# A four-layer graph network on one core: operands filled to 128 rows and columns, readers after all writers of a bank, and a new order

## The chip, the cores and the metric

The kernel runs on one core of a Trainium2 chip. The metric is the device time of one execution in microseconds (us): the median of the runs, 2941.53 us before the change (3 runs, 2940.82 to 2942.3).

A core has five engines with a queue of instructions each: TensorE (PE in the profile; PEld is its loading of weights), VectorE (DVE), ScalarE (ACT), GpSimd (POOL) and SyncE (SP), which only issues DMAs here. TensorE writes to PSUM, eight banks of 128 x 512 fp32; VectorE and ScalarE read them.

## The reference

There are B = 32 graphs with 512 nodes of 128 features and a 512 x 512 adjacency of zeros and ones (3% ones). Four layers follow each other, each on relu(layernorm(x)) = h and each added to x:

```python
# layer 0: p = h @ (W1 - W2), q = h @ W2; maximum over a node's neighbours
x = x + max_j(relu(p[i] + q[j] + b) * adj[i, j])
# layer 1: four inner layers, with earlier inputs concatenated to the third's and fourth's
src = nodes @ ws + bs;  src_agg = l2norm(adj, rows) applied to src
dst = nodes @ wd + bd;  dst_agg = l2norm(adj, columns), transposed, applied to dst
nodes = tanh(concat(src_agg, nodes @ wn + bn, dst_agg) @ wu + bu)
# layer 2: rows of adj divided by their sums
x = x + (adj / rowsum) @ (h @ weight) + bias
# layer 3: four gated recurrent (GRU) steps with m = adj.T @ (h @ weight[l])
r, z = sigmoid(...), sigmoid(...);  n = tanh(xn + r * hn);  h = (1 - z) * n + z * h
```

## The kernel before

**One graph after another, six at a time.** `batch(b)` writes down the work of one graph: `load`, `prepare` (layer 0's projections, the transposed adjacency `at`, the neighbours' ranks `ccd`, row and column sums), `gathers` (layer 0's maximum), `layer1`, `layer23`. Nothing is issued there: `F.vec`, `F.act`, `F.pool`, `F.sync`, `F.mm` and `F.tr` only note operations in a `Flow`. `Flow.run` is a planner that works when the program is built. It keeps up to AHEAD = 6 parts (the weights' three parts, then graphs) open, and picks instruction after instruction: of those whose inputs and buffers are ready first on an engine, the one with the earliest due time. So each engine's queue is a fixed order in which several graphs' work is mixed, and TensorE's products of one graph fill another's waits. The profile gives nearly all work the line of the call in `Flow.step`, L510.

**Due times.** An operation's due time is its graph's place times `PACE`, less the planned length of what follows it in its graph, less its stage's `LEADS`: a higher lead means earlier. `FIRST` and `LAST` shift the places of the first and last graphs, `WEIGHTS` are the places of the weights' parts. The costs in `Flow.cost` are the planner's own estimates. `spaced` keeps the maxima of gathered rows SPACING apart. Where the planner sees a long gap on TensorE it puts in "spin" products, whose result nobody reads.

**Banks.** All products go to eight PSUM banks, which four groups share: group 0 is `prepare`, 1 is `layer1`, 2 is layers 2 and 3, 3 is `gathers`. `BANKS` says how many each group is sure of; the rest are spare, for any group.

**Layer 0.** For rank k = 1 to 4, `oh` marks where a half of the nodes has its k-th neighbour, and `pa = qhl.T @ oh` fetches that neighbour's q by a product; VectorE takes the maximum into `acc`. The neighbours that are left (up to seven a node) are fetched by indirect DMAs, `G<-qtab,idx`, into the maximum `gm`.

**Layer 1.** The features are split into an fp32r high part and a low part, `hi` and `lo`, which are multiplied by the exact 0/1 matrices `at` and `an` into `pg`; `ag` is `pg` times the norms `rbc`. All weights of an inner layer are multiplied together ahead of time, so that `pu` sums fp32 products of features (`f`, `hT`) and aggregates (`ag`). What the biases `bs` and `bd` add depends on the node through its sums of the normalized adjacency: that is one fp32r product of the weights `b8` (8 x 128: high and low parts) and `rows` (8 x 512), the first into each `pu`:

```python
F.mm(flat(pu), W.b8[:, i, :], rows, start=True, stop=False)
```

`rows` comes from `sc`, six columns of scalars for each node (four of them the high and low parts), which GpSimd computes in `prepare`, TensorE transposes (`psc`, a tile of 128 x 24), ScalarE copies to `sct`, and SP writes to DRAM and reads back as rows.

**Layer 2.** `po` is one bank with four fp32 products, one for each 128 nodes; VectorE reads each of its quarters into `x` (x3 in the code). The tile framework keeps a bank's writers and readers apart by waits, in the order in which they were issued; the planner sees only each quarter.

**Layer 3.** In each step l, `pk` are the two gates, `pg` the aggregate that ScalarE copies to `mT`, `phn` and `pxn` the candidate's two products; `ph` is the transposed new state, of which `hi` and `lo` are made for the next step, or `xo` at the end. Only the last graph (`own`) is cut in halves of 256 nodes (`cuts`), takes its banks from group 0 and its buffers from stages that are done, so that it overlaps with the one before it. Its halves share the bank of `phn` (with `pxn` in the same bank) and that of `ph`.

Of the kernel before, what the change touches and what calls it, by code (L numbers as in the profile page):

```python
# [24 lines left out]
P = 128  # L25
# [8 lines left out]
NLEFT = 7  # L34
PACE = 45.35
SPACING = 1.8
AHEAD = 6
BANKS = (2, 1, 2, 1)

LEADS = {  # L40
    "prepare": -33.2, "counts": -28.6, "keys": -38.2, "rows": -9.6,
    "gather0": 12.6, "gather1": -3.5, "gather2": -1.7, "gather3": -10.5,
    "first": 14.4, "layer1": -15.5, "layer10": -39.2, "layer11": -39.2,
    "layer12": -26.1, "layer13": -57.9, "layer2": 50.7, "layer3": 187.5,
    "layer30": 155.2, "layer31": 193.8, "layer32": 81.5, "layer33": 66.2,
    "out": 33.8,
}
FIRST = (-0.01, -0.0, -0.31, 0.0)
LAST = (0.0, -0.23, -0.17, -0.97, -0.05)
WEIGHTS = (-5.87, -1.69, -2.33)  # L50

# [204 lines left out]
class Engine:  # L256
# [5 lines left out]
    def __getattr__(self, op):  # L262
        fn = getattr(self.real, op)

        def note(*args, **kw):
            outs, ins = [], []
            for i, v in enumerate(args):
                (outs if i == 0 else ins).append(v)
            for k, v in kw.items():
                (outs if k in ("out", "accum_out") else ins).append(v)  # L270
            ins = [v.ap if isinstance(v, Rows) else v for v in ins]
            outs, ins = ([v for v in vs if hasattr(v, "free_size")] for vs in (outs, ins))
            cost, after = self.flow.cost(self.name, op, outs, ins)
            self.flow.note(self.name, fn, args, kw, outs, ins, cost, after)


            tensors = [v for v in ins if v.free_size() >= 64 and in_sbuf(v)]
            fast = self.name == "vec" and op == "tensor_scalar" and outs[0].free_size() > 256
            if self.name == "vec" or (self.name == "pool" and op.startswith("tensor")):
                self.flow.part[-1].port = fast or len(tensors) > 1  # L280

        return note


class Flow:
# [50 lines left out]
    def cost(self, engine, op, outs, ins):  # L336

        aps = outs + ins
        n = max(a.free_size() for a in aps)
        o = outs[0].free_size()  # L340
        if "dma" in op:
            if engine != "pool":
                width = 2 if outs[0].dtype == BF16 else 4
                return 0.48 if engine == "sync" else 0.42, 2.0 + outs[0].size() * width / 1.2e5
            return (1.25, 6.0) if "indirect" in op else (0.7, 4.0)
        if engine == "vec":
            if op == "tensor_scalar" and o > 256:
                t = o / 1920.0 + 0.157
            elif op == "bn_stats":
                t = 0.28  # L350
            else:
                t = (o if op != "max" else n) / 960.0 + 0.15
                if op == "scalar_tensor_tensor" and len(ins) == 3:
                    t += 0.06
            return t - 0.082 + (0.08 if len(outs) > 1 else 0.0), 0.082
        if engine == "act":
            t = o / 1200.0 + 0.16 + 0.1 * (len(ins) - 1) + (0.04 if in_sbuf(ins[0]) else 0.0)
            return t - 0.1 + (0.2 if len(outs) > 1 else 0.0), 0.1
        if op == "tensor_tensor" and o < 64:
            return 1.1 if o < 8 else 1.7, 0.0  # L360
        two = op in ("tensor_tensor", "tensor_add", "tensor_sub", "tensor_mul")
        return (o / 408.0 + 0.05 if two and o > 64 else o / 1100.0 + 0.18), 0.0
# [35 lines left out]
    def mm(self, out, lhsT, rhs, start, stop, group=None):  # L398

        n = rhs.free_size()  # L400
        if rhs.dtype == F32:
# [7 lines left out]

    def tr(self, out, in_, ident):  # L410
        self.note(
            "pe", self.nc.tensor.transpose, (out, in_, ident), {}, [out], [in_, ident],
            0.109 if in_.dtype == F32 else 0.056, 0.16,
# [190 lines left out]
class FastWeights:  # L604
# [5 lines left out]
    def __init__(self, nc, F, a, const, mid, ps):  # L610
# [47 lines left out]
        nc.gpsimd.memset(self.sign[0:4, 1:2], 0.0)  # L658
        self.nc, self.a, self.const, self.n = nc, a, const, n

    def own(self, shape, dtype, name):
        return self.F.tile(self.const, shape, dtype, name, name)

    def temp(self, tag, name, wide=False):
# [27 lines left out]
    def rest(self):  # L692
# [30 lines left out]

        self.b8 = self.own([8, NL1, P], F32R, "b8r")
        bm = self.own([P, NL1, 2, 8], F32, "bm")
# [5 lines left out]
        for i in range(NL1):  # L731
# [24 lines left out]
            for k in range(2):  # L756
# [10 lines left out]
            F.vec.scalar_tensor_tensor(  # L767
                self.b8[:, i, :], hi.bitcast(F32), self.sign[0:8, 0:1], full, ALU.mult, ALU.add
            )
# [53 lines left out]
def fast(ctx: ExitStack, tc: tile.TileContext, a: dict, out: bass.AP, bad):  # L823
# [12 lines left out]
    F.share(ps, 8, {f"ps{s}": n for s, n in enumerate(BANKS)} | {"idle": 0})  # L836

    def bank(s, shape, dtype, name):
        return F.tile(ps, shape, dtype, f"ps{s}", name, BANKS[s])

# [54 lines left out]

    def transposed(s, src, name):

        pt = pst(s, name)
        for t in range(NT):
            F.tr(pt[:, t, :], src[:, t, :], W.ident)  # L900
        return pt

# [7 lines left out]

    def parts(s, src, tag, buf=plain, cuts=(slice(None),)):

        hi = buf(F32R, f"hi{s}", f"hi_{tag}")
        lo = buf(F32R, f"lo{s}", f"lo_{tag}")
        for c in cuts:
            v, h, l = ((w if len(cuts) == 1 else w[:, c, :]) for w in (src, hi, lo))
            F.act.copy(h, v)
# [13 lines left out]
    def prepare(b, xt, af):  # L931
# [60 lines left out]
        for t, (first, step) in enumerate(CODES):  # L992
            F.sync.dma_start(
                out=tab[first : first + (P - 1) * step + 1 : step, :], in_=qn[:, t, :]
            )
        F.lead = LEADS["counts"]

# [14 lines left out]

        F.lead = LEADS["keys"]


        dm = F.tile(small, [P, 2, NT], F32, tag="dm", name=f"dm_{b}", bufs=4)
        F.pool.tensor_scalar(dm, deg, 1.0, None, ALU.max)
        sc = F.tile(small, [P, 6, NT], F32, tag="sc", name=f"sc_{b}", bufs=4)
        F.pool.tensor_tensor(
# [34 lines left out]
        pt = pst(0, f"psc_{b}")  # L1054
        F.tr(pt[0 : 6 * NT, 0, :], sc.rearrange("p k t -> p (k t)"), W.ident)
        sct = F.tile(small, [6 * NT, P], F32, tag="sct", name=f"sct_{b}", bufs=1)
# [6 lines left out]
    def gathers(b, at, ccd, qhl, pn, tab, idx, has, dinv):  # L1063
# [15 lines left out]
        for jt in range(NT):  # L1079
            F.lead = LEADS[f"gather{jt}"]  # L1080
            for k in range(1, KSLOT + 1):
                oh = F.tile(big, [P, 2, N], F32R, tag="oh", name=f"oh_{b}_{jt}_{k}", bufs=3)
                F.vec.tensor_scalar(oh, ccd[jt], NBASE + k, None, ALU.is_equal)
                for u in range(2):
# [4 lines left out]
                    else:  # L1089
                        F.vec.tensor_max(acc, acc, flat(pa))  # L1090
        F.lead = LEADS["first"]
        pt = transposed(3, acc.rearrange("p (t q) -> p t q", q=P), f"px_{b}")
# [15 lines left out]
    def layer1(b, x1, an, at, dinv):  # L1108
# [5 lines left out]
        F.sync.dma_start(out=rbc, in_=scal[0:2, :].unsqueeze(0).to_broadcast([P, 2, N]))  # L1114
        rows = F.tile(mid, [8, N], F32R, tag="rows", name=f"rows_{b}")

        xn = norm(1, x1, f"{b}_1")
        two = sbuf_parts(1, xn, f"{b}_1")
        F.act.copy(rows, row8)
        pt = transposed(1, xn, f"pt_{b}_1")  # L1120
# [5 lines left out]
        for i in range(NL1):  # L1126
            F.lead = LEADS[f"layer1{i}"]
            names = INPUTS[i]
# [10 lines left out]
            pu = pst(1, f"pu_{b}_{i}")  # L1139
            F.mm(flat(pu), W.b8[:, i, :], rows, start=True, stop=False)  # L1140
            late = []
# [13 lines left out]
            feat[new] = fi  # L1155
        F.lead = LEADS["layer2"]
        pt = transposed(1, feat[new], f"px_{b}_2")
# [5 lines left out]
    def layer23(b, x2, an, at, dinv):  # L1163
# [16 lines left out]
        for t in range(NT):  # L1180
            F.mm(po[:, t, :], mT[:, t, :], W.w2, start=True, stop=True)
        x3 = x2
        F.lead = LEADS["layer3"]
        for t in range(NT):
# [15 lines left out]
        for l in range(W.NL3):  # L1200
            F.lead = LEADS[f"layer3{l}"]
            gates = []
# [42 lines left out]
            else:  # L1245
                halves = [(v[:, 0:step, :], v[:, step:NT, :]) for v in phn]
            pt = pst(s, f"ph_{b}_{l}")
            for c, (vh, vx) in zip(cuts, halves):
                F.mm(flat(vh), W.gh[l][:, 2, :], flat(cut(h, c)), start=True, stop=True)
                F.vec.scalar_tensor_tensor(  # L1250
                    cut(nn, c), vh, W.bhh[:, n : n + 1], cut(r, c), ALU.add, ALU.mult
                )
                F.mm(flat(vx), W.gm[l][:, 2, :], flat(cut(mT, c)), start=True, stop=True)
                F.vec.tensor_add(cut(nn, c), vx, cut(nn, c))
# [7 lines left out]
                for t in range(c.start, c.stop):  # L1262
                    F.tr(pt[:, t, :], hn[:, t, :], W.ident)
            h = hn
            if l + 1 < W.NL3:
                two = parts(2, pt, f"{b}_3_{l}", buf, cuts)
        F.lead = LEADS["out"]
        xo = buf(F32, "mT", f"xo_{b}")
        for t in range(NT):
            c = b * NT + t  # L1270
            F.vec.scalar_tensor_tensor(
                xo[:, t, :], pt[:, t, :], W.mcol[:, c : c + 1], x3[:, t, :], ALU.mult, ALU.add
            )
# [3 lines left out]
    def batch(b):  # L1277
        F.lead = LEADS["prepare"]
        one = prepare(b, *load(b))
        F.lead = LEADS["rows"]  # L1280
        one = gathers(b, *one)
        F.lead = LEADS["layer1"]
        layer23(b, *layer1(b, *one))
# [486 lines left out]
```

## Time and profile before

| What | Before |
|---|---|
| Median of 3 runs | 2941.53 us |
| Profiled execution | 2943.54 us |
| Its span, first to last instruction | 2941.8 us |
| Instructions | 37748 |
| Granted TensorE clock, mean | 0.993 of full speed |
| PE products, busy | 2843.4 us, 11493 |
| VectorE, busy | 2384.2 us, 5382 |
| ScalarE, busy | 1218.1 us, 2547 |
| GpSimd, busy | 1827.3 us, 2013 |
| The 8-row product `pu<-rows,b8r` | 128, mean 493 ns |
| The transposition `psc<-ident,sc` | 32, mean 273 ns |
| Layer 2's `po<-w,mT` | 256 passes, mean 288 ns in the table by form |

The span is the time between the first and the last instruction of the profiled execution, which lasted 1.7 us longer. A row like `PE pu<-ag,w 128*128 128x512` names the engine, the tile that is written, what it is made from, the weights' shape (rows*columns) and the moving operand's shape. An fp32 product runs as two passes and shows as two instructions. A matmul's record overlaps with the next one's: what it costs is read from start to start.

### The profile page before, as it was taken

To read this page: it belongs to the slowest core of one execution; us is meant where nothing else is said; L and a number is where in the kernel's file an instruction comes from. 1 tells how busy PE (TensorE), PEld (TensorE's weight loads), DVE (VectorE), ACT (ScalarE), POOL (GpSimd) and SP (SyncE) were. 2 spreads that over 40 slices of the span, in tenths; PEclk is the share of its full clock that TensorE was granted. 3 is DMA by queue.
4 is the path that set the end of the run, shared out by engine and by line. 5 is a ranking of instruction groups with operands and counts; after the bars stand their busy time and mean duration, and the time that the engine had idled before them with its cause. 6 is when DMAs were issued, how large, how long until landed. Compare 5 with 4: busy or idle time off the path is not lost.

```text
span 2941.8 us, 37748 instructions
## 1 busy us (share of the span) xinstructions
PE 2843.4 (97%) x11493; PEld 1753.8 (60%) x11513; DVE 2384.2 (81%) x5382; ACT 1218.1 (41%) x2547; POOL 1827.3 (62%) x2013
## 2 busy tenths in 40 slices
PE   7899999999999999999999999999999999999997
PEld 3555556666666566666666566666666666555555
DVE  6988878888888898888888888889888888887533
ACT  2434434434444344344444444444344444333323
POOL 4676667666666666666666666666666666565312
PEclk8999999999999999999999999999999999999999
DMA  7642434334334334333433433343333333342100
GB/s 154 145 91 48 84 69 86 85 72 81 65 66 86 85 74 86 59 72 80 86 85 73 84 61 65 86 87 77 80 68 69 75 86 84 56 77 37 33 4 9
DMA packets 191267, 218.44 MB, mean 74 GB/s; under 512 B 30376, under 2 KB 139600, under 8 KB 191056
## 3 DMA queue, kind: packets, MB, share of 16 engines
q0 software_dynamic: 47104, 92.34, 22.2%
q1 hardware_dynamic: 73768, 63.63, 7.4%
q10 hardware_dynamic: 70184, 59.98, 6.7%
q8 instruction: 93, 1.52, 0.2%
q14 instruction: 118, 0.97, 0.1%
HBM read 164.32 MB, written 17.96 MB: 62 GB/s over the span
## 4 chain that ended last, share of the span: by engine, by line
PE 80%; DVE 10%; issue 4%; DMA 2%; ACT 2%; POOL 1%; ACTq 0%; SPq 0%; DVEq 0%; POOLq 0%
PE pg L510 25%; PE pu L510 19%; PE pk L510 15%; PE pa L510 6%; PE phn L510 4%; PE pxn L510 3%; DVE acc L510 3%; PE pkey L510 2%; PE ph L510 2%; PE pf L510 2%; PE po L510 1%; DMA G<-qtab,idx 1%; DVE nn L510 1%; PE pt L510 1%; DVE x L510 1%
## 5 line engine op out<-in xcount | busy, mean ns | idle before, releaser
L510 POOL DMA_INDIRECT G<-qtab,idx x768 | 848.6, 1105 | 589.6 <-DVE gm L510 453.3
L510 DVE TENSOR_TENSOR acc<-acc,pa 128x512 f32<-128x512 f32 x992 | 673.6, 679 | 146.4 <-PE pa L510 134.5
L510 PE MATMUL pa<-oh,qhl 128*128 128x512 f32 x1024 | 465.7, 510 | 11.2 <-DVE oh L510 5.3
L510 PE MATMUL pg<-an,hi 128*128 128x512 f32 (+1 forms) x1040 | 457.3, 441 | 0.6 <-DVE acc L510 0.4
L510 PE MATMUL pu<-ag,w 128*128 128x512 f32 x896 | 448.0, 592 | 0.5 <-DVE ag L510 0.3
L510 PE MATMUL pg<-an,lo 128*128 128x512 f32 (+1 forms) x1040 | 436.0, 422 | 0.0
L510 DVE TENSOR_SCALAR oh<-ccd 128x1024 fp32r<-128x1024 bf16 x512 | 393.9, 787 | 13.3 <-PE pa L510 13.2
L510 PE MATMUL pg<-at,lo 128*128 128x512 f32 x640 | 295.9, 462 | 0.8 <-DVE lo L510 0.4
L510 PE MATMUL pg<-at,hi 128*128 128x512 f32 x640 | 281.1, 439 | 7.2 <-DVE acc L510 1.8
L510 PEld LDWEIGHTS pa<-oh,qhl 128*128 128x128 f32 x1024 | 193.9, 191 | 152.2 <-issue 40.4
L510 ACT ACTIVATE xn<-x,shift,rstd 128x128 f32<-128x128 f32 x512 | 211.5, 484 | 171.6 <-POOL shift L510 170.1
L510 DVE TENSOR_TENSOR gm<-gm,G 128x128 f32<-128x128 f32 x768 | 253.4, 331 | 8.7 <-DMA G<-qtab,idx 7.7
L510 PE MATMUL pk<-h,g_hh 128*128 128x512 f32 (+1 forms) x528 | 256.3, 590 | 0.6 <-DVE top L510 0.6
L510 PEld LDWEIGHTS pg<-an,hi 128*128 128x128 f32 x1040 | 195.1, 188 | 93.2 <-issue 49.1
L510 PEld LDWEIGHTS pg<-an,lo 128*128 128x128 f32 x1040 | 195.2, 188 | 84.7 <-issue 40.3
L510 PE MATMUL pk<-mT,g_ih 128*128 128x512 f32 (+1 forms) x528 | 242.3, 580 | 1.4 <-ACT mT L510 1.1
L510 ACT ACTIVATE gate<-pk,bsum 128x512 f32<-128x512 f32 (+1 forms) x264 | 176.9, 673 | 140.8 <-PE pk L510 137.3
L510 PEld LDWEIGHTS pu<-ag,w 128*128 128x128 f32 x896 | 168.1, 189 | 110.9 <-issue 80.0
L510 POOL TENSOR_TENSOR rstd<-rstd,mhalf 128x4 f32<-128x4 f32 x128 | 139.8, 1092 | 138.8 <-DVE shift L510 133.6
L510 DVE TENSOR_TENSOR ag<-pg,rbc 128x512 f32<-128x512 f32 x256 | 174.8, 684 | 61.3 <-PE pg L510 58.5
L510 ACT COPY mT<-pg 128x512 f32<-128x512 f32 (+1 forms) x164 | 94.2, 575 | 304.6 <-PE pg L510 300.0
L510 ACT CAST hi<-ph 128x512 fp32r<-128x512 f32 (+1 forms) x99 | 56.8, 574 | 341.2 <-PE ph L510 333.4
(172 smaller groups left out, 5110.4 us busy)
## 6 DMA issues: line engine op xcount, KB each, us to landing
af<-in_adj_dram ACTq DMA_DIRECT2D x32, 1024.0 KB
ccd<-cc SPq DMA_DIRECT2D x512, 64.0 KB
an<-in_adj_dram POOLq DMA_DIRECT2D x128, 256.0 KB, 3.9
x<-in_x_dram ACTq DMA_DIRECT2D x64, 256.0 KB
rbc<-scal SPq DMA_DIRECT2D x32, 512.0 KB
G<-qtab,idx POOLq DMA_INDIRECT x768, 3.8
qtab<-qn SPq DMA_DIRECT2D x128, 64.0 KB
out_dram<-xo ACTq DMA_DIRECT2D x32, 256.0 KB
```

What stands on the lines that cost most here:

```text
L510: op.fn(*(real(v) for v in op.args), **{k: real(v) for k, v in op.kw.items()})
```

## The change

It does four things.

- **Filled operands.** `b8` becomes 128 x 4 x 128 and `rows` 128 x 512, filled with zeros once at the start; only their first 8 partitions are written afterwards. `rows` is one fixed buffer instead of a tile of its own ring, which had one buffer too. `sc` becomes the first 24 columns of one of two fixed 128 x 128 tiles (`vectors`, zero elsewhere), and the whole tile is transposed.
- **Layer 2's projections.** The four products into `po` are noted as writers of the whole bank, so that the planner issues every reader after all of them.
- **Halves.** In the last graph each half's `ph` has its own bank, and both products of a half's candidate are issued before their first reader.
- **The order.** New `PACE`, `SPACING`, `BANKS`, `LEADS`, `FIRST`, `LAST` and `WEIGHTS`; the first and the last graph get leads of their own, which are added to the stage's. [...]

```diff
-PACE = 45.35
-SPACING = 1.8
+PACE = 47.93
+SPACING = 1.5
-BANKS = (2, 1, 2, 1)
+BANKS = (2, 1, 3, 1)
 LEADS = {
...
-    "layer12": -26.1, "layer13": -57.9, "layer2": 50.7, "layer3": 187.5,
-    "layer30": 155.2, "layer31": 193.8, "layer32": 81.5, "layer33": 66.2,
-    "out": 33.8,
+    "layer12": 4.8, "layer13": -92.9, "layer2": -3.0, "layer3": -37.4,
+    "layer30": 11.6, "layer31": 120.9, "layer32": 146.5, "layer33": 18.4,
+    "out": 39.3,
 }
-FIRST = (-0.01, -0.0, -0.31, 0.0)
-LAST = (0.0, -0.23, -0.17, -0.97, -0.05)
-WEIGHTS = (-5.87, -1.69, -2.33)
+LEADS0 = {
...
+LEADSN = {
...
+    "layer12": 77.8, "layer13": 256.2, "layer2": 230.7, "layer3": 341.4,
+    "layer30": 205.3, "layer31": 82.3, "layer32": 56.8, "layer33": 15.6,
...
+FIRST = (9.02, 0.15, 0.05, 0.0)
+LAST = (0.0, -0.06, -0.82, -0.98, -9.3)
+WEIGHTS = (-8.07, -5.76, -16.24)
...
+    def lead(b, stage):
+        own = LEADS0 if b == 0 else LEADSN if b == B - 1 else {}
+        return LEADS[stage] + own[stage] if stage in own else LEADS[stage]
...
-            fast = self.name == "vec" and op == "tensor_scalar" and outs[0].free_size() > 256
+            fast = self.name == "vec" and op == "tensor_scalar"
...
-            return (1.25, 6.0) if "indirect" in op else (0.7, 4.0)
+            return (1.05, 6.0) if "indirect" in op else (0.7, 4.0)
...
+        self.rows = self.zeros([P, n // P, P], "rows")
+        self.vectors = []
+        for i in range(2):
+            t = fixed([P, P], F32, f"vectors{i}")
+            nc.gpsimd.memset(t, 0.0)
+            self.vectors.append(F.fixed(t, [P, P], F32))
...
+    def zeros(self, shape, name):
+        t = self.const.tile(shape, F32R, name=name)
+        for k in range(shape[1]):
+            self.nc.vector.tensor_scalar(t[:, k, :], self.ident, 0.0, None, ALU.mult)
+        return self.F.fixed(t, shape, F32R)
...
-        self.b8 = self.own([8, NL1, P], F32R, "b8r")
+        self.b8 = self.zeros([P, NL1, P], "b8r")
...
-        sc = F.tile(small, [P, 6, NT], F32, tag="sc", name=f"sc_{b}", bufs=4)
+        full = W.vectors[b % 2]
+        sc = full[:, 0 : 6 * NT].rearrange("p (k t) -> p k t", t=NT)
...
-        F.tr(pt[0 : 6 * NT, 0, :], sc.rearrange("p k t -> p (k t)"), W.ident)
+        F.tr(pt[:, 0, :], full, W.ident)
...
-        F.act.copy(rows, row8)
+        F.act.copy(flat(W.rows[0:8]), row8)
...
-            F.mm(flat(pu), W.b8[:, i, :], rows, start=True, stop=False)
+            F.mm(flat(pu), W.b8[:, i, :], flat(W.rows), start=True, stop=False)
...
-            F.mm(po[:, t, :], mT[:, t, :], W.w2, start=True, stop=True)
+            F.mm(po[:, t, :], mT[:, t, :], W.w2, start=True, stop=True, group=po)
...
-            pt = pst(s, f"ph_{b}_{l}")
-            for c, (vh, vx) in zip(cuts, halves):
-                F.mm(flat(vh), W.gh[l][:, 2, :], flat(cut(h, c)), start=True, stop=True)
+            pts = [pst(s, f"ph_{b}_{l}_{c.start}") for c in cuts]
+            for c, (vh, vx), bank_, pt in zip(cuts, halves, phn, pts):
+                bank_ = bank_ if len(cuts) > 1 else None
+                F.mm(
+                    flat(vh), W.gh[l][:, 2, :], flat(cut(h, c)), start=True, stop=True, group=bank_
+                )
+                F.mm(
+                    flat(vx), W.gm[l][:, 2, :], flat(cut(mT, c)), start=True, stop=True, group=bank_
+                )
                 F.vec.scalar_tensor_tensor(
                     cut(nn, c), vh, W.bhh[:, n : n + 1], cut(r, c), ALU.add, ALU.mult
                 )
-                F.mm(flat(vx), W.gm[l][:, 2, :], flat(cut(mT, c)), start=True, stop=True)
```

`LAST` has five entries of which the code uses the first four: those of the last four graphs.

## The prediction

> **What bounds the kernel now.** I read the page first: which engine is full, and where.
>
> ```profile
> PE 2843.4 (97%) x11493; PEld 1753.8 (60%) x11513; DVE 2384.2 (81%) x5382; ACT 1218.1 (41%) x2547; POOL 1827.3 (62%) x2013
> PE   7899999999999999999999999999999999999997
> DVE  6988878888888898888888888889888888887533
> ```
>
> TensorE is full in all but the first and last slice, VectorE never for long. The chain that ended last, in order of time, shows how regular it is:
>
> ```profile
> 1141.88 3.19 PE pu L510 x7
> ...
> 1228.43 3.19 PE pu L510 x7
> ...
> 1314.99 3.19 PE pu L510 x7
> ```
>
> The same piece comes back every 86.55 us, a batch's period. 32 periods are 2770 us; 172 of the span's 2941.8 us lie in the filling and draining ends. The stages by time:
>
> ```profile
> 50.00:100.00 50.00, 42.02 (x205) 22.85 (x206) 46.23 (x112) 15.06 (x41) 34.62 (x42) 0.84 0.84 137
> 1000.00:2000.00 1000.00, 990.80 (x4032) 617.44 (x4031) 849.97 (x1921) 436.53 (x907) 656.86 (x718) 1.00 0.37 75
> 2900.00:2942.00 42.00, 27.72 (x144) 20.36 (x145) 14.41 (x35) 11.45 (x28) 6.92 (x12) 0.90 0.05 15
> ```
>
> Columns: window, length, then busy time of PE, PEld, DVE, ACT, POOL, granted clock, DMA share, GB/s. In the middle PE is busy 99%, so only time that PE's own instructions lose can shorten a batch. "Busy" hides such losses, as matmuls overlap; start-to-start times show them:
>
> ```profile
> 1434.20 0.83 PE L510 MATMUL po<-w,mT 128*128 128x128 f32 x6
> 1435.55 0.49 PE L510 MATMUL po<-w,mT 128*128 128x128 f32 x2 [0.51 <-DVE x L510]
> 1435.79 0.48 PE L510 MATMUL pg<-at,lo 128*128 128x512 f32 x1
> ...
> 1437.04 0.39 PE L510 MATMUL pg<-an,lo 128*128 128x512 f32 x1
> 1437.27 0.39 PE L510 MATMUL pg<-at,hi 128*128 128x512 f32 x1
> 1437.59 0.49 PE L510 MATMUL pu<-rows,b8r 8*128 8x512 f32 x1
> 1438.01 0.50 PE L510 MATMUL pg<-an,hi 128*128 128x512 f32 x1
> 1438.34 0.39 PE L510 MATMUL pg<-at,lo 128*128 128x512 f32 x1
> 1438.57 1.02 PE L510 MATMUL pu<-f,w 128*128 128x512 f32 x2
> ...
> 1444.99 0.22 PE L510 MATMUL pkey<-code,at 128*128 128x128 bf16 x1
> 1445.05 0.27 PE L510 MATMUL psc<-ident,sc 128*24 128x128 f32 x1
> 1445.27 1.98 PE L510 MATMUL pk<-h,g_hh 128*128 128x512 f32 x4
> ```
>
> A full-height fp32r product of 512 columns steps 0.23 us (1437.04 to 1437.27). Around the 8-row product the steps are 0.32, 0.42 and 0.33.
>
> **Part 1, b8 and rows to 128 rows.** The three steps 1437.27 to 1438.34 take 1.07 us; three full-height ones take 0.69. The 8-row product costs 0.38 us too much: its weight load does not go ahead of the product before it, nor the next load ahead of it. With 128 rows it is of the form of pc<-at,lt or pg<-an, which step 0.23 among their like. Four a batch, 128 in all: 0.38 x 128 = 49 us. Five fall before 200 us, where VectorE (46.2 of 50 us) and not PE sets the pace, and a few in the drain: I take 46. From below, if only the product's own step (0.42 to 0.23) and the one before it mend: 0.28 x 120 = 34. The copy into rows still writes 8 partitions (620 ns), so the wait for it stays.
>
> [...]
>
> **Part 2, psc to 128 columns.** The narrow transposition steps 0.22 us (1445.05 to 1445.27); a full-width one (four ph<-ident in 0.44 us, 1404.68 to 1405.12) steps 0.11. 32 x 0.11 = 3.5 us; I take 3. From 0 (its load grows from 93 to 141 ns and might show) to 7, if the next instruction is delayed likewise.
>
> **Part 3, layer 2's projections together.** po's four fp32 products (eight passes) share a bank with the readers x. In 31 batches the readers stand between them:
>
> ```profile
> PE po L510 <- DVE x L510: 16.0, 31, 1.0
> ```
>
> 1434.20 to 1435.79 is 1.59 us for eight passes that would take 8 x 0.11 = 0.87: 0.72 lost, times 31 is 22 us. Below: the idle time alone, 16. With all four products ahead of the readers that wait cannot arise. The first x comes some 0.3 us later for its own batch, beside some 80 us of other batches' work.
>
> **Part 4, banks for halves.** Only the last batch is cut in halves. Its second half's ph at 2919.30 starts after the first half's lo (ready 2919.24), though its h was ready at 2918.55: some 0.6 us a layer. At the end the same with xo: 0.45 us. Four places, 2 us, and phn's products ahead of the reader some 1: I take 3. Against it, BANKS keeps three for layer 3 and leaves one spare where two were; the last batch (group 0, two kept) can hold three banks instead of four, and a second pg3 may wait for the first's mT (0.37 us) in four layers, some 2 us. Range -2 to +3.
>
> **Part 5, setup.** Eight zero fills on VectorE by the row code<-ident,fcode (0.28 us at most, 2.2 us) fall in its idle 10.7 us before 17.06; two GpSimd fills of 0.20 fall in its idle 18.2 us before 20.92. Nothing; 2.6 us if that cover were gone.
>
> **Part 6, order and leads.** Everything moves: gathers and an loads on GpSimd's queue, ccd and rbc loads on SP's, products between batches. In the middle each queue has room: GpSimd 66% busy, ACT 44%, DMA share 0.37, so a moved load finds its queue free, and six open batches give TensorE other work. What new order can win is at the ends. After the second last out (issued 2899.88) the last one runs alone until 2931.36, 31 us for three layers of some 11 us, chain-bound with spin products in the gaps. Earlier urgency for the last batch could share some of it, at most 25 us; a last batch that displaces the one before it loses as much. No row prices it; I take -6, nearer to none than to either end, because filling is held by VectorE (92 to 94% busy between 50 and 150 us), which no order shortens.
>
> Sum against the profiled execution (2943.5 us, span 2941.8): 46 + 3 + 22 + 3 + 6 = 80, giving 2863.5. The median stands 2.0 below that execution: 2861. The period falls by 4 x 0.38 + 0.72 + 0.11 = 2.35 to 84.2 us.
>
> **The rivals.**
>
> A, slower: the spare bank. Gathers' pa keeps one bank plus one spare instead of two. Pairing every pa with the acc that reads it between 400 and 2500 us, 242 of 769 start while two or more earlier are still unread: ten a batch that the new limit forbids. If TensorE waited an acc (0.68 us) for each, a batch would pay 6.8 us against 2.35 won; from 35% of these waits on, the kernel is slower, and at half it is 32 x 1.05 = 34 us, 2975. For: VectorE takes the acc at 0.68 us, three times pa's step. Against: PE waited for acc before pa only 8 times (4.0 us), and an order made with the limit can put other products between.
>
> B, it doesn't do what it says: the long steps belong to this operand's place or the wait for rows, not its height. Then only parts 2 to 6 remain, 34 us: 2908. Against: four different neighbours, always the same three steps; the wait for rows appears only 5 times (7.0 us).
>
> C, VectorE becomes the bound. Its 850 us per 1000 are 73.6 us a batch, 87% of 84.2; with waits in between, an order that keeps it only at the 85% of today would hold the period at 86.5, and at 86% gives 85.6, some 2905. Against: it ran at 94% between 100 and 150 us.
>
> D, the end leads pay fully: 25 us instead of 6, 2842. For: the last slice is PE's emptiest (27.7 of 42 us). Against: each of its steps waits for the one before.
>
> **How the numbers follow.** Forecast 0.66, D 0.10, B 0.10, C 0.05, A 0.09. The best of all terms (49 + 7 + 22 + 3 + 25 = 106) gives 2835; all lower ends with an order that loses 25 (34 + 0 + 16 - 2 - 25 = 23) give 2919. I set 2835 to 2912: it takes in B, C and D and leaves out A and the worst sums. The forecast's own range is 2840 to 2890. 0.2% (6 us) is what a measurement of this kernel can tell. Faster: all but A and a few sums that cancel, 0.89; same 0.02; slower 0.09.
>
> **What would show it.** pu<-rows reads 128*128 and steps 0.23; no PE wait of po for x; the recurring piece every 84.2 us; VectorE at 87% between 1000 and 2000 us. Wrong: a period above 85.5, PE waits on acc before pa of more than 1 us a batch (A), long steps still around rows (B), or more than 172 us outside 32 periods.

## The result: slower, and the profile after

The changed kernel takes 2974.61 us (median of 4 runs, 2973.22 to 2982.38) against 2941.18 beside it. The ratio, estimated from all runs together, is 1.0121 with an interval of 1.0102 to 1.0141; the two medians alone give 1.0114. The forecast was 2861, and its range ended at 2912. The profiled execution lasts 2973.2 us with a span of 2971.4.

The page after, busy time and VectorE's slices, and the same stretches by time:

```profile
PE 2819.8 (95%) x11515; PEld 1772.1 (60%) x11515; DVE 2319.9 (78%) x5390; ACT 1202.4 (40%) x2547; POOL 1881.3 (63%) x2015
...
DVE  6888878787888778878888888778788778877634
```

```profile
1000.00:2000.00 1000.00, 964.01 (x3911) 609.75 (x3910) 809.39 (x1864) 414.68 (x874) 665.06 (x699) 0.99 0.38 75
2929.00:2971.00 42.00, 30.88 (x145) 22.07 (x143) 18.22 (x41) 13.79 (x29) 8.31 (x12) 0.90 0.05 15
```

In the middle PE is busy 964 us of 1000 instead of 991, at a clock of 0.99 instead of 1.00. VectorE fell too, from 850 to 809, so it is not the bound: the engines wait for each other. The recurring piece of the chain now stands so:

```profile
1118.40 3.67 PE pu L528 x9
1206.88 3.67 PE pu L528 x9
```

That is 88.5 us apart, where 84.2 was forecast. Over the outs between 480 and 2480 us the mean period is 88.73 us; before, 86.72. Outside of 32 periods lie 132 us; before, 167. So, by this count, the ends won 35 us, and the middle lost 64. (The count takes all 32 graphs at the middle's period; the last five of the changed kernel come faster, so part of both numbers cancels, see e13 below.) At the very end the last two outs stand 5.3 us apart, where they stood 31.5 before.

The edits do on TensorE what they should. Around the rows product in the timeline after:

```profile
1014.12 0.39 PE L528 MATMUL pg<-at,lo 128*128 128x512 f32 x1
1014.35 0.40 PE L528 MATMUL pg<-an,lo 128*128 128x512 f32 x1
1014.58 0.40 PE L528 MATMUL pu<-rows,b8r 128*128 128x512 f32 x1
1014.82 1.02 PE L528 MATMUL pu<-f,w 128*128 128x512 f32 x2
```

The steps are 0.23, 0.23 and 0.24; the 0.32, 0.42 and 0.33 are gone here. No wait of po for x is left among the waits. But two waits have grown, of the gates' pk for mT and of ph for h. Before, then after (us in total, times, longest):

```profile
PE pk L510 <- ACT mT L510: 1.1, 3, 0.6
PE ph L510 <- DVE h L510: 7.3, 11, 1.4
...
PE pk L528 <- ACT mT L528: 44.1, 23, 2.0
PE ph L528 <- DVE h L528: 21.6, 33, 1.6
```

Behind one of these 2.0 us stands this row of queues (GpSimd, ScalarE and TensorE of the timeline after):

```profile
1503.06 1.58 POOL L528 TENSOR_TENSOR rstd<-rstd,mhalf 128x4 f32<-128x4 f32 x1
1504.30 1.20 POOL L528 DMA_INDIRECT gm<-qtab,idx  x1
1505.53 1.93 POOL L528 TENSOR_TENSOR shift<-shift,rstd 128x4 f32<-128x4 f32 x1
...
1507.50 1.65 ACT L528 ACTIVATE xn<-x,shift,rstd 128x128 f32<-128x128 f32 x4 [5.22 <-POOL shift L528]
1509.05 0.56 ACT L528 COPY mT<-pg 128x512 f32<-128x512 f32 x1
...
1509.67 1.98 PE L528 MATMUL pk<-mT,g_ih 128*128 128x512 f32 x4 [2.00 <-ACT mT L528]
```

The new order puts a gather between the second norm's `rstd` and its `shift` on GpSimd in 29 of 32 graphs. From rstd's start to shift's end it takes 4.40 us. ScalarE stands at xn for 5.22 us. mT, of another graph, waits behind xn in ScalarE's queue although its pg is done at 1505.71, 3.3 us before mT starts, and TensorE waits for mT. Over the run ScalarE waits 272.5 us for shift (170.1 before).

The gather is only a part of this lateness. While shift runs, VectorE is in a check of the adjacency, and shift ends 0.06 us after it:

```profile
1505.13 2.27 DVE L528 SCALAR_TENSOR_TENSOR junk<-af 128x2048 bf16<-128x2048 f32 x1
```

So it is in all 23 places where shift runs beside `junk<-af`: it takes 1.75 to 1.94 us and ends 0.05 or 0.06 us after it. Behind 22 of them, some 2 us later, stands one of the waits of pk for mT, and these are all of the 23 waits but one of 0.24 us. In 7 of the 29 graphs with a gather in between, `junk<-af` runs at another time: shift takes 0.20 to 0.51 us there, and no such wait follows. In the order of before `junk<-af` never meets a shift, and the 37 shifts right behind a gather take 0.20 to 0.22 us:

```profile
1511.46 1.87 POOL L510 DMA_INDIRECT G<-qtab,idx  x1 [0.20 <-issue]
1513.36 0.22 POOL L510 TENSOR_TENSOR shift<-shift,rstd 128x4 f32<-128x4 f32 x1
```

Some of the waits cost more than themselves. The timeline and the windows of after at another one:

```profile
1064.23 3.67 PE L528 MATMUL pk<-mT,g_ih 128*128 128x512 f32 x4 [1.99 <-ACT mT L528]
```

```profile
1064.00:1068.00 4.00, 3.77 (x5) 1.65 (x6) 0.75 (x1) 2.07 (x6) 2.23 (x2) 0.57 0.04 7
```

The same four products that took 1.98 us above take 3.67 here, at a granted clock of 0.57. Between 500 and 2400 us, 7 of 20 waits of 2.0 us for mT are followed by such a drop, in which twelve instructions take 6.36 instead of 4.66 us. The mean clock of the run is 0.988 against 0.993: an estimate of 0.005 x 2971 = 15 us for all such drops.

### The profile page after: what moved, and what is told of

Same layout as the page of the kernel before. It is cut to its first block, busy times and chain, and to the rows that moved or that the text cites. A ratio compares the mean times of both kernels' runs of the same rounds, so it can differ in the third digit from the quotient of the medians.

```text
span 2971.4 us, 37817 instructions
## 1 busy us (share of the span) xinstructions
PE 2819.8 (95%) x11515; PEld 1772.1 (60%) x11515; DVE 2319.9 (78%) x5390; ACT 1202.4 (40%) x2547; POOL 1881.3 (63%) x2015
## 4 chain that ended last, share of the span: by engine, by line
PE 63%; POOL 15%; DVE 8%; issue 5%; ACT 4%; DMA 3%; SPq 0%; ACTq 0%; POOLq 0%; DVEq 0%
PE pg L528 18%; PE pu L528 16%; PE pk L528 11%; PE pa L528 5%; POOL G L528 4%; POOL gm L528 3%; PE pxn L528 3%; POOL rstd L528 3%; PE phn L528 2%; POOL shift L528 2%; DVE acc L528 2%; ACT xn L528 2%; DMA G<-qtab,idx 2%; PE ph L528 2%; PE pq L528 2%
## 5 line engine op out<-in xcount | busy, mean ns | idle before, releaser
L528 POOL DMA_INDIRECT G<-qtab,idx x768 | 821.4, 1070 | 660.7 <-DVE gm L528 382.8
L528 PE MATMUL pa<-oh,qhl 128*128 128x512 f32 x1024 | 482.6, 521 | 22.1 <-ACT mT L528 6.4
L528 PE MATMUL pg<-an,hi 128*128 128x512 f32 (+1 forms) x1040 | 476.2, 459 | 3.8 <-DVE acc L528 0.4
L528 DVE TENSOR_SCALAR oh<-ccd 128x1024 fp32r<-128x1024 bf16 x512 | 347.3, 693 | 12.5 <-PE pa L528 8.7
L528 ACT ACTIVATE xn<-x,shift,rstd 128x128 f32<-128x128 f32 x512 | 216.9, 484 | 272.7 <-POOL shift L528 272.5
L528 PE MATMUL pk<-mT,g_ih 128*128 128x512 f32 (+1 forms) x528 | 257.8, 610 | 44.1 <-ACT mT L528 44.1
L528 DVE TENSOR_TENSOR gm<-gm,G 128x128 f32<-128x128 f32 x768 | 235.3, 308 | 32.9 <-DMA G<-qtab,idx 31.3
L528 PE MATMUL pg<-at,lo 128*128 128x512 f32 x640 | 255.6, 399 | 3.9 <-POOL lo L528 2.0
L528 DVE SCALAR_TENSOR_TENSOR nn<-phn,bcol,gate 128x512 f32<-128x512 f32 (+1 forms) x132 | 96.7, 733 | 161.7 <-ACT gate L528 161.3
L528 POOL TENSOR_TENSOR rstd<-rstd,mhalf 128x4 f32<-128x4 f32 x128 | 166.9, 1304 | 76.9 <-DVE shift L528 70.7
L528 POOL TENSOR_TENSOR lo<-xn,hi 128x512 fp32r<-128x512 f32 x96 | 123.5, 1287 | 143.5 <-ACT hi L528 103.8
```

The source lines that it names most:

```text
L528: op.fn(*(real(v) for v in op.args), **{k: real(v) for k, v in op.kw.items()})
```

## The experiments

To part the edits from the order, an order is written down once and replayed. `Flow.step` no longer chooses, it takes the next one of a constant list:

```diff
     def step(self):
-        best = None
...
+        key = ORDER[self.turn]
+        op = next(o for e in self.ENGINES for o in self.waiting[e] if o.key == key)
```

Ratios are to the kernel before on the same chip, from all runs together, with the 95% interval; periods are of the profiled execution.

| Run | Median, us | Before beside it | Ratio | Period, us |
|---|---|---|---|---|
| changed | 2974.61 | 2941.18 | 1.0121 (1.0102 to 1.0141) | 88.73 |
| e1 | 2896.24 | 2946.72 | 0.9829 (0.9813 to 0.9846) | 85.06 |
| e2 | 2918.39 | 2946.72 | 0.9904 (0.9887 to 0.9920) | 85.87 |
| e3 | 2923.99 | 2946.72 | 0.9922 (0.9905 to 0.9939) | 85.96 |
| e4 | 2907.83 | 2946.72 | 0.9865 (0.9848 to 0.9881) | 86.31 |
| e5 | 2941.64 | 2945.59 | 0.9986 (0.9976 to 0.9995) | 87.14 |
| e6 | 2996.72 | 2945.59 | 1.0175 (1.0158 to 1.0192) | 89.01 |
| e7 | 2893.39 | 2945.59 | 0.9823 (0.9807 to 0.9839) | 84.78 |
| e8 | 3061.16 | 2945.59 | 1.0390 (1.0372 to 1.0407) | 90.65 |
| e9 | 2914.97 | 2944.73 | 0.9897 (0.9880 to 0.9913) | 85.93 |
| e10 | 2852.21 | 2944.73 | 0.9681 (0.9665 to 0.9697) | 84.07 |
| e11 | 2910.31 | 2944.73 | 0.9880 (0.9864 to 0.9897) | 86.30 |
| e12 | 2967.37 | 2942.60 | 1.0082 (1.0069 to 1.0096) | 88.96 |
| e13 | 2898.75 | 2942.60 | 0.9854 (0.9839 to 0.9869) | 85.60 |
| e14 | 2958.67 | 2945.27 | 1.0047 (1.0030 to 1.0064) | 88.67 |
| e15 | 2921.65 | 2945.27 | 0.9920 (0.9907 to 0.9933) | 86.70 |
| e16 | 2873.51 | 2940.83 | 0.9773 (0.9759 to 0.9787) | 84.95 |

### The edits in the order of before (e1, e2, e3)

e1 replays the order of before with rows and b8 of 128 rows, psc of 128 columns (four zero-filled tiles, as sc had buffers) and po's four products ahead of the readers; e2 has rows and b8 alone, e3 po alone.

```diff
-            F.mm(flat(pu), W.b8[:, i, :], rows, start=True, stop=False)
+            F.mm(flat(pu), W.b8[:, i, :], flat(W.rows), start=True, stop=False)
```

```diff
-            F.mm(po[:, t, :], mT[:, t, :], W.w2, start=True, stop=True)
+            F.mm(po[:, t, :], mT[:, t, :], W.w2, start=True, stop=True, group=po)
```

> The kernel before with its own issue order written out and replayed, plus the filled operands (rows, b8, and sc in four zero-filled tiles) and layer 2's four products ahead of their readers; no halves' banks, no new constants. Theory O (the new order alone lost the time; the edits are worth what the prediction said): 46 + 3 + 22 = 71 us less, 2870, in a range of 2860 to 2890, period 84.2 us. Theory E (the edits bring nothing on the path, other waits take the time over): 2925 to 2945.

> The same replayed order with only b8 and rows filled to 128 rows. Theory O: 46 us less than before, 2895 (34 to 49 less, 2892 to 2907). Theory E: within 10 us of before.

> The same replayed order with only layer 2's four products moved ahead of their first reader. Theory O: 22 us less, 2919 (16 to 22 less). Theory E: within 5 us of before, the late first reader costing what the wait did.

The edits win 50.5 us, between the two theories and nearer to O; alone, rows and b8 win 28.3 (less than the 34 to 49 of theory O) and po 22.7. So the edits are sound and the order loses: 1.0121 / 0.9829 = 1.030, about 86 us. (e1 lacks the halves' banks of the changed kernel, which touch the last graph alone.) Of the profiled executions' 77.7 us of difference, the middle has 32 x 3.67 = 117 us against e1 and the ends give 40 back. Of the 3.67, about 2.5 are idle time of PE (3.3 a graph against 0.8 between 480 and 2480 us) and about 0.6 the clock.

The rows term is 18 us short of its 46, though TensorE's own part came in full: over all 128 rows products the median steps before, of and behind them fell from 0.32, 0.42 and 0.53 us before to 0.23, 0.24 and 0.43 in the changed kernel, together 0.37 us as the prediction had it. In e1 ph waits for h in more places than before, and there is a new wait for lo:

```profile
PE ph L511 <- DVE h L511: 13.6, 30, 2.1
...
PE pg L511 <- POOL lo L511: 6.5, 22, 0.3
```

### One instruction's place on GpSimd, on ScalarE (e4, e5, e7)

e4 is the changed kernel with every shift right behind its rstd on GpSimd (92 moved). e5 leaves that and puts mT ahead of xn on ScalarE where it stands right behind (27 places). e7 is e1 with e4's move (69 places).

```diff
  rstd_14_1
+ shift_14_1
  gather gm_15
- shift_14_1
  lo_14_1
```

```diff
+ mT
  xn (four parts)
- mT
```

> The changed kernel with its own issue order replayed, except that on GpSimd each norm's small product shift comes right behind its rstd, ahead of the gathers and other work that the new order puts between them (92 places); nothing else differs. Theory O1 (a late shift holds ScalarE's queue at xn, and mT behind it keeps TensorE waiting): the wait of pk for mT (44 us) and part of that of ph for h (22 us) go, 30 to 60 us less than the changed kernel, 2915 to 2945. Theory O2 (the loss of the new order lies elsewhere: spare bank, products between batches): within 10 us of the changed kernel, 2965 to 2985.

> The changed kernel with its own issue order replayed, except that on ScalarE, in 27 places, a copy mT that stands right behind a norm's four xn goes ahead of them; GpSimd's order is the changed kernel's, gathers between rstd and shift included. Theory Q (the late shift hurts only through ScalarE's queue: xn waits at its head, mT stands behind it): the wait of pk for mT (44 us, some 2.2 us a batch with its weight loads) goes, 40 to 60 us less than the changed kernel, 2915 to 2935; the wait of ph for h stays. Theory G (GpSimd is late for everybody, and what xn feeds is late next): less than 20 us gained, 2955 to 2975.

> The first experiment's kernel (order of before replayed, filled operands, layer 2's readers after all products) with each norm's shift right behind its rstd on GpSimd as well (69 places, mostly layer 2's and 3's norms). If the late shift also costs this order something: 5 to 25 us less than the first experiment, 2871 to 2891 at its chip's pace. If there the late shift is hidden by six open batches: within 5 us of it, 2891 to 2901.

e4's timeline (GpSimd, then ScalarE) at the same pair of operations:

```profile
1470.98 1.59 POOL L529 TENSOR_TENSOR rstd<-rstd,mhalf 128x4 f32<-128x4 f32 x1
1472.65 0.20 POOL L529 TENSOR_TENSOR shift<-shift,rstd 128x4 f32<-128x4 f32 x1
...
1472.88 1.65 ACT L529 ACTIVATE xn<-x,shift,rstd 128x128 f32<-128x128 f32 x4 [2.67 <-POOL shift L529]
```

rstd's start to shift's end takes 1.87 instead of 4.40 us, pk's wait for mT is gone, and so are the drops of the clock between 500 and 2400 us. In its new place shift is also done before `junk<-af` starts (at 1473.06 here), so the move takes away the gather and the meeting with `junk<-af` at once. The ratio falls from 1.0121 to 0.9865, about 75 us, more than the 30 to 60 expected, for an operation of 128 x 4. e5 wins 40 us without touching GpSimd; 25 shifts still meet `junk<-af` there, but pk's wait for mT falls to 1.9 us: the place in ScalarE's queue is a link of the same chain. In the order of before e4's move changes nothing (e7 against e1, within the intervals).

### Undoing an edit in the new order, and the old constants (e6, e8)

e6 is the changed kernel, in its own order, with 8-row operands again. e8 has the changed kernel's edits, plans anew, and takes all order constants of before.

```diff
-            F.mm(flat(pu), W.b8[:, i, :], flat(W.rows), start=True, stop=False)
+            F.mm(flat(pu), W.b8[0:8, i, :], flat(W.rows[0:8]), start=True, stop=False)
```

```diff
-PACE = 47.93
-SPACING = 1.5
-BANKS = (2, 1, 3, 1)
+PACE = 45.35
+SPACING = 1.8
+BANKS = (2, 1, 2, 1)
...
```

> The changed kernel with its own issue order replayed, but the product of b8 and rows uses only their first 8 partitions again. If every 8-row product costs TensorE its 0.38 us wherever it stands: 46 us more than the changed kernel, 3020. If part of it falls into waits that the new order has anyway (PE busy only 96% there): 20 to 40 us more, 2995 to 3015.

> The changed kernel with all constants of the order set back (PACE, SPACING, BANKS, LEADS, FIRST, LAST, WEIGHTS, no leads of their own for the first and last graph, the planner's two costs), and planned anew with the edits in place. If the constants make the order: as the first experiment, 2885 to 2905. If the constants fit one plan alone, and the edits' few other dependencies (rows a fixed buffer, po one group) throw the planner onto another path: slower than both kernels, 3000 to 3120.

The 128-row operands are worth only 0.54% in the new order, 16 us (uncertain by some 8, from the two intervals), below the 20 to 40 expected: where TensorE waits for mT, time saved on TensorE turns into waiting. e6 shows it: its waits for mT are of 1.7 us instead of 2.0 (41.0 us in 25 places), and none of the 21 between 500 and 2400 us is followed by a drop of the clock. With e8 the edits lose 3.9%, as expected for constants that fit one plan alone. An order belongs to one list of operations, so "the edits with the old constants" is no measure of the edits; the replay is.

### GpSimd relieved in the order of before, and spin products (e9, e10, e11)

e9 is the kernel before, e10 is e1, both without the sixth and seventh left neighbours' gathers and maxima. e11 is e4 without the planner's spin products between 400 and 2500 us.

```diff
+                if r >= NLEFT - 2:
+                    F.part[-1].fn = lambda *args, **kw: None
```

```diff
-            if self.spin and gap > self.IDLE and n > 0:
+            if self.spin and gap > self.IDLE and n > 0 and not 400.0 < t < 2500.0:
```

> The kernel before, order replayed, without the sixth and seventh of the left neighbours' gathers and their maxima (8 of 28 gathers on GpSimd and 8 of 24 maxima on VectorE per graph left out). If TensorE alone sets the pace there: the period stays at 86.5 us, within 10 us of before.

> The first experiment's kernel (old order, edits) with the same gathers and maxima left out. The edits won 50 us there instead of 71. Theory V (the rest is kept by waits for VectorE and GpSimd, whose work for h, lo and the maxima comes too late once TensorE is quicker): with these two relieved the edits win 62 to 75 us against the same kernel without edits, period 84.2 to 84.5 us. Theory M (an 8-row product's long steps are not all lost time, the term itself is smaller): 45 to 55 us, period about 85.0.

> The fourth experiment's kernel (new order, shift right behind rstd) without the spin products that the planner puts in between 400 and 2500 us of its own time (about one pair a graph). If they delay the product behind them: 5 to 20 us less than the fourth experiment, 2888 to 2903. If TensorE waits there for h anyway: within 5 us of it.

e9 was a miss: it wins 29.8 us, where at most 10 were expected if TensorE alone sets the pace, and its period is 0.8 us shorter. So even before, with TensorE busy 99% of the middle, waits for GpSimd's and VectorE's work were part of the period.

With fewer gathers the edits are worth 62.8 us (2914.97 to 2852.21) instead of 50.5, just within theory V: 12 us of what e1 lacked come back when GpSimd and VectorE are relieved. So part of the shortfall lies with these engines, whose results come too late once TensorE is faster; by the runs' intervals the 12 us are uncertain by some 8. The spin products cost nothing that shows (0.9880 against 0.9865).

### Why fewer gathers don't help the new order (e12 to e16)

e12 leaves the same gathers out of the changed kernel. e13 has both moves of e4 and e5. e14 is e12 with the first norm's rstd and shift ahead of zc on GpSimd, in 23 graphs. e15 has all gathers and all three moves, e16 all three moves and fewer gathers.

```diff
  gm_14
+ rstd_17_0
+ shift_17_0
  zc_12_0
  gather G_15_3_1
- rstd_17_0
  gate1_12_0
  x1_14
- shift_17_0
  gather gm_15
```

> The changed kernel and its own order, the sixth and seventh left neighbours' gathers and their maxima left out (8 of a graph's 28 gathers). In the order of before this saved 30 us, with the edits in it 44 us. If the new order's loss is lateness that comes out of GpSimd's queue of gathers, it saves clearly more here, 60 to 110 us: 2864 to 2914 us, ratio 0.973 to 0.989 against before, ScalarE's wait for shift at half of its 272 us or less. If the loss lies elsewhere (ScalarE's own order, the banks), it saves the 30 to 44 us that it saved there: 2930 to 2944 us, ratio 0.995 to 1.000.

> The changed kernel's order with both moves: shift right behind rstd on GpSimd, and mT ahead of the norm's xn on ScalarE. If both moves mend the same link (xn late because shift is late, mT late because it stands behind xn), the second adds nothing to the first: ratio 0.9865 within 0.2 points, about 2906 us. If ScalarE's queue delays mT for a reason of its own, the second adds a good part of the 40 us that it won alone: 2870 to 2890 us, ratio 0.975 to 0.981.

> As the run before without the sixth and seventh gathers in the new order, and on GpSimd the first norm's rstd and shift of 23 graphs go ahead of zc, so that a gather stands between them and gate and x. Without this, rstd, gate, x and shift follow each other and VectorE's nn<-nn,zc of that time takes 4.04 us instead of 0.69 (87 us too much over 400 to 2500 us, 27 in the changed kernel); TensorE's ph then waits 1.6 us a graph for h (40 us) and its granted clock falls for some 4 us after such a wait. If that run of GpSimd's operations is what took the gain back, the 87 us fall to 30 or less, ph<-h to 20 or less, the drops of the clock mostly go, and the time falls by 25 to 60 us: 2907 to 2942. If nn is held for another reason or the wait moves on to another pair, the time stays within 10 us of 2967.

> The changed kernel with all its gathers and three moves in its order: this move of the first norm's rstd and shift (23 graphs), every other shift right behind its rstd, mT ahead of xn. If what is left of the new order's cost (a period of 85.60 us with the two other moves, 85.06 with the same edits in the order of before) is VectorE held at nn and ph waiting for h (15.6 us), it is faster than the two moves alone by 5 to 15 us: ratio 0.980 to 0.984. If not, it stays at 0.9854 within 0.2 points.

> The new order with the sixth and seventh gathers and their maxima left out and all three moves: the first norm's rstd and shift ahead of zc, every shift right behind its rstd, mT ahead of xn. Without the last two moves the mT wait was 47.6 us, with 19 drops of the clock. If the new order has two places where TensorE waits (mT behind a late xn; h behind a held nn), and mending one lets the other decide, then with both mended fewer gathers save at last what they saved in the order of before: 30 to 44 us below the same moves with all gathers (2921.65), 2878 to 2892 us, ratio 0.977 to 0.982, and no drops of the clock. If the order is late in still other places, less than 15 us: above 2906.

| Run | pk waits for mT, us | ph waits for h, us | mean nn<-nn,zc, ns | mean clock |
|---|---|---|---|---|
| before | 1.1 | 7.3 | 763 | 0.993 |
| changed | 44.1 | 21.6 | 951 | 0.988 |
| e12 | 7.9 | 40.3 | 1428 | 0.982 |
| e13 | 0.2 | 15.6 | 893 | 0.992 |
| e14 | 47.6 | 7.1 | 884 | 0.982 |
| e15 | 0.2 | 27.1 | 898 | 0.992 |
| e16 | 1.3 | 7.3 | 876 | 0.993 |

e12 missed both expectations: it saves 0.4%, not 30 us or more. mT's wait nearly goes, though a gather still stands between rstd and shift in 29 graphs: `junk<-af` now meets only 6 shifts. But the time goes to h and acc:

```profile
PE ph L529 <- DVE h L529: 40.3, 32, 1.9
PE pa L529 <- DVE acc L529: 26.6, 27, 1.2
```

e12's timeline shows what h stands behind (GpSimd's rows first, then VectorE's and TensorE's):

```profile
1136.55 1.37 POOL L529 TENSOR_TENSOR rstd<-rstd,mhalf 128x4 f32<-128x4 f32 x1
1137.91 1.27 POOL L529 TENSOR_TENSOR gate<-h,gate 128x512 f32<-128x512 f32 x1
1139.15 1.28 POOL L529 TENSOR_TENSOR x<-gm,x 128x512 f32<-128x512 f32 x1
...
1136.94 4.04 DVE L529 TENSOR_TENSOR nn<-nn,zc 128x512 f32<-128x512 f32 x1
...
1143.48 0.69 DVE L529 TENSOR_TENSOR h<-gate,nn 128x512 f32<-128x512 f32 x1
...
1144.22 0.48 PE L529 MATMUL ph<-ident,h 128*128 128x128 f32 x1 [1.62 <-DVE h L529]
```

nn<-nn,zc takes 4.04 us, where 0.69 is usual, and ends 0.55 us after the third of GpSimd's operations. acc and h stand behind it in VectorE's queue. It is so in 20 places of e12, always beside this row of GpSimd's. So nn lasted through three operations in a row. The times alone don't show that the row is the cause: e14 tests it.

e14 takes that row apart and moves nothing else. nn falls to 884 ns and ph's wait from 40.3 to 7.1 us, as expected, but `junk<-af` meets 26 shifts again, mT's wait is back at 47.6 us with the drops of the clock, and the time falls by only 0.35%: half of its expectation held, and the time was a miss. So the new order is late in two places: in e12 TensorE waits at the one, in e14 at the other. e16 mends both: 2873.51 us, no drop of the clock between 400 and 2400 us, a period of 84.95. That is 1.5 points of the ratio below e15 and 0.8 below e13: with both mended, fewer gathers pay at last, as expected against e15; against e13 they pay 24 us, less than the 30 to 44. The same edits and fewer gathers in the order of before (e10, 0.9681) are still 0.9 points faster. Fewer gathers with the two moves of e13 alone were not tried, so whether e16 needs the third move is not shown.

In e13 the second move added nothing to the first (0.9854 and 0.9865), so both mend one link. Most of the order's loss is this link: e13 stands 0.25 points of the ratio above e1, the changed kernel 2.9. e15 was a miss: with all gathers the third move costs 0.7%, since on GpSimd zc now stands behind rstd and shift, nn waits for zc (21.9 us in 24 places, 1.1 in e13), and ph's wait rises from 15.6 to 27.1 us.

The best version with the whole computation is e7, 0.9823, which e1 equals within the intervals: the edits in the order of before.

## Why the prediction was wrong

**The step that failed is Part 6.** It costed the new order's middle at nothing because "In the middle each queue has room: GpSimd 66% busy, ACT 44%, DMA share 0.37, so a moved load finds its queue free, and six open batches give TensorE other work". The first half took shares over 1000 us for the state of a queue at one moment: GpSimd is 67% busy in the same window after, and shift still ends 4.40 us after rstd begins, behind a gather and beside VectorE's `junk<-af`, 0.06 us after its end. The second half forgot that every queue here is a fixed order: whatever of other graphs stood behind pk in TensorE's queue had to wait with it, and ScalarE had mT ready behind xn and could not take it. The runs showed in its place 22 waits of some 2 us for mT and the drops of the clock behind some of them; moving shift alone gives 75 us back (e4). The measured term is +86 us (order and end leads together) where -6 was set and +25 was the worst end; by the profiled executions, counted with 32 periods, +117 in the middle and -40 at the ends.

The premise ahead of all parts was too strong as well: "In the middle PE is busy 99%, so only time that PE's own instructions lose can shorten a batch". e9 leaves out work of GpSimd and VectorE alone and wins 29.8 us, most of it in the middle (0.8 us a period).

**Part 6's other half** had the right sign. The 40 us of the ends against e1 hold some 25 that belong to the middle: the last five graphs lack its waits, but are counted at its period. In e13, the same order without the waits for mT, the ends take 157 us against e1's 172: 15 us, where 6 was set and 25 allowed. The last graph's out follows the one before it after 5.3 us instead of 31.5, which is the sharing that Part 6 named; filling got no shorter, as it said (in e13 the sixth out comes at 743 us, before at 730). D's reason held, but could not save the sum. Its cause among LEADS0, LEADSN, FIRST and LAST was not tried alone.

**Part 1** named the right mechanism: the three long steps went, so B falls. With 8 rows the product's weight load starts with the product (at 1437.58 and 1437.59 us; 2 ns ahead in the median of the 128), with 128 rows together with the product before it (at 1014.35, the rows product at 1014.58; 229 ns ahead in the median). TensorE's own 0.37 us a product came in full. The term was mis-sized: 28 us in the order of before (23 to 33 by the interval), 16 in the new one, instead of 46. Counting steps priced TensorE's own time and took it as time of the kernel; the forecast kept VectorE's and GpSimd's results as early as they were, and e1's waits for h and lo show that they were just in time before. Rival C is out for the changed kernel, whose VectorE is busy 81% of the middle, but not for what e1 lacks: there it is busy 87%, where C put its limit at 85 or 86, and e10 relieves VectorE and GpSimd at once, so it doesn't part a full engine from a late one.

**Part 3** held: 22 was set, 22.7 measured, and the wait is gone.

**Parts 2, 4 and 5** are too small to part: e1 is e2's and e3's gains together (51.0 us) within 1 us, so 3 us for psc is neither shown nor refuted. The halves' banks were not tried alone.

**Rival A** named a time, 2975, that came true, by a mechanism that did not: pa's waits for acc grew only from 4.0 to 5.9 us. Agreement with a number is not agreement with a cause.

**The signs given beforehand** did their work: a period above 85.5 was to show the forecast wrong, and did at once; "more than 172 us outside 32 periods" did not occur (132). A sign for waits of TensorE other than po's and pa's was missing, and there the time went.

**Still open.** e13's period is 0.5 us above e1's and 0.8 above e7's. That `junk<-af` lengthens shift is read from their times alone: it was not moved by itself. A gather between rstd and shift doesn't by itself cost time: the order of before has 37 of them, and e7, which moves them, gains nothing. The planner's two changed estimates (`fast` and the 1.05 of an indirect DMA in the diff) were not changed alone, so which of the constants made this order is not known.

## What to carry to other kernels

When a change comes with a new static order, price the order on its own: replay the old order with the edits and the new order without one link, and don't set the order's term at nothing: here it was larger (86 us) than the edits' (50). An engine that is 65% busy is no cover for a moved instruction: ask what stands directly behind it in its in-order queue, which engine waits for that, and what the neighbouring engine does at that moment. If relieving one engine doesn't shorten the run, list the waits again before dropping the theory: two late places in one loop can hide each other, until both are mended.

## What the hardware showed beyond expectation

- A wait of TensorE of 2.0 us was followed in 7 of 20 places of the changed kernel (500 to 2400 us) by some 3.4 us at half the granted clock (0.50 between 1064.39 and 1067.79 us), 1.7 us more (6.36 against 4.66 us for twelve instructions). In e14 19 of 22 waits of 2.0 us were followed by a drop, in e6 none of 21 waits of 1.7 us. What parts the waits with a drop from those without was not shown.
- GpSimd's shift, where it started while VectorE's `junk<-af` (2.27 us) ran, ended 0.05 or 0.06 us after it and took 1.75 to 1.94 instead of 0.20 us, in 23 of 23 places of the changed kernel. In the kernel before, the 29 instructions of GpSimd (plain DMA issues aside) that start during `junk<-af` all end after it.
- VectorE's `nn<-nn,zc` took 3.4 us longer beside three GpSimd operations that followed each other (4.04 against 0.69 us), in 20 places of e12; with the row taken apart (e14) its mean fell from 1428 to 884 ns.
- The product `pu<-rows,b8r` cost more with 8 rows between 128-row products than with 128: in the median the steps before, of and behind it were 0.32, 0.42 and 0.53 us in the order of before and 0.23, 0.24 and 0.43 in the changed kernel. Filling it with zeros won 28 us of 2947 in one order and 16 in another.
